# Four reorderings at the end of an attention and mixture-of-experts kernel: row scatters, lists, normalisations and token loads

## The chip, the cores and the metric

The kernel runs on one core of a Trainium2 chip. The metric is the device time of one launch in microseconds (us), the median of several runs. One further launch is recorded by the hardware profiler; all views of the profile are of that launch, and their times count from the start of its span.

## What is computed

The input is x, 4 sequences of 512 tokens with 256 features, and for each sequence 8 condition values. All is float32. Cut to what matters (c for the condition values):

```python
# one of 8 gated networks per sequence, chosen by the largest condition value
h = (silu(x @ wu.T + bu) * (x @ wg.T + bg)) @ wd.T + bd
# attention, 16 heads of width 16 that share one key and one value head
p = softmax(q @ k.T);  o = p @ v
x = x + o @ Wo.T + bo
# per sequence a weight mixed from 8 masked ones
z = x @ mix(c, weight * mask).T + bias
# routing in 8 groups of 256 tokens: each token goes to the best two of 8 experts,
# at most 128 places per expert and group; the rest is dropped
probs = softmax(z @ w_router);  top 2;  place = running count per expert
out = sum over a token's experts of probs * (gelu(z @ wi[e]) @ wo[e])
x = x + out
```

## The kernel before, in words

**Stages.** The first stage runs the gated networks for all sequences. The second walks through 64 steps n, 16 for each sequence b (k = n mod 16). A step computes four exponentiated score tiles on the scalar engine (`exponentials`, L409), takes the row maxima of a tile six steps ahead on the vector engine (`maxima`, L379), and multiplies the exponentials of the step before with the values (`weigh`, L423). Four steps make a unit of attention; its result is copied out of PSUM (L432) and stored to a buffer in memory, `od` (L433). The third stage runs the experts' networks.

**Work beside the attention steps.** The rest of a sequence is cut into pieces, which `finish(b)` builds and the lists `beside` and `last` hand out: entry k names the pieces of step k, with the sequence they belong to as an offset (-1 is the sequence before). `values` loads the attention results and their sums (L444, L448), `inv` takes the reciprocal (L473), stores it and loads it again spread over the partitions (L474, L478), `norm0` and `norm1` multiply (L486), `out0` to `out3` are the output projection with the residual (L503, L508, stored by L509), `rT` transposes (L524), `mix` multiplies with the mixed weight (L535), `choose` and `rank0`, `rank1` pick the two experts (L552 to L583), `places`, `rows` and `send` count places (L601 to L650). `row0` to `row3` each issue two scatters (L656): GpSimd DMAs that write 128 rows of 264 numbers to the places of `to_i` in a buffer `xp`, which is sorted by expert. In all but the last sequence a scatter also waits for the last `weigh` issued so far.

**Units of experts' work.** A unit is 256 rows of one expert (a pair) or 128 or fewer (singles and smaller ones). Which expert and which rows is known only at run time: `list_of_pairs` and `lists_of_rest` compute tables on the vector engine (L827 to L903), and SyncE reads them. The first two units come from the first two sequences, units 2 to 5 (N0 = 2 to NA = 6) after three, the rest after the last. For a unit u, `fetch_rows(u)` loads its rows from `xp` (L934), `fetch_in(u)` and `fetch_out(u)` its two weights of 1 MB (L912, three buffers each), `turn(u)` transposes the rows on the tensor engine (L978) and copies them back on the vector engine (L980), `up(u, half)` is the first product with gelu (L1051, L1055), `put(u, h)` the second (L1084), weighted by L1094 and added to the output by a GpSimd DMA (L1098). An add waits for the add of the unit before.

**What sets the order.** The program's text: each engine and each of SyncE's, ScalarE's and GpSimd's DMA queues executes in the order in which the instructions were written, and each instruction waits for the semaphores of what it depends on. So a SyncE load that waits for something holds up the loads written after it. `fetch_rows` of units 0 and 2 waits for all scatters so far, and that of the first unit of the rest for all of them.

**The passage from steps to units.** In the last sequence, `pairs0` to `pairs6` begin the third stage: `pairs2` loads unit 0's first weight and the rows of units 0 and 1, `pairs4` loads `fetch_in(1)` and `fetch_out(0)`, `pairs5` is `turn(0)`, `pairs6` is `fetch_in(2)` and `fetch_out(1)`. After the last step, `up(0, 0)` comes, then the last `weigh`, and `run(units, ..., begun=True)` takes over. In `run`, iteration k works on unit k's first product and unit k-1's second, loads rows of unit k+2 (`rows_behind`), `fetch_in` of unit k+3 and `fetch_out` of unit k+2. Between them it calls `place()`, and the n-th call does the pieces of the last sequence that `final` lists under n; `"rest"` there stands for `lists_of_rest`. Loads of units whose table isn't written yet are kept in `late` until it is.

Of the kernel before, what the change touches and what calls it, by code (L numbers as in the profile page):

```python
# [18 lines left out]
B = 4  # L19
# [17 lines left out]
N0, NA, NB, NSURE, NNEXT, NHALF, NQUARTER = 2, 6, 5, 10, 18, 2, 2  # L37
# [5 lines left out]
def adaln_attn_ffn_kernel(  # L43
# [22 lines left out]
    nc = tc.nc  # L66
    mm = nc.tensor.matmul
# [632 lines left out]
    def route_mixed(b):  # L700
# [39 lines left out]
    ]  # L740
    last = [
        [(-2, "rank0")],
        [(-2, "rank1")],
        [(-1, "values"), (-2, "places"), (-2, "rows")],
        [(-1, "inv"), (-2, "send")],
        [(-2, "row0")],
        [(-1, "norm0"), (-1, "norm1"), (-2, "row1")],
        [(-1, "out0"), (-1, "out1"), (0, "pairs0"), (-1, "out2"), (-1, "out3"), (-2, "row2")],
        [(-1, "rT0"), (-1, "rT1"), (-2, "row3")],
        [(-1, "mix0"), (-1, "mix1"), (0, "pairs1"), (-1, "mix2"), (-1, "mix3")],  # L750
# [1 line left out]
        [(-1, "rank1"), (0, "pairs2")],  # L752
        [(-1, "places"), (-1, "rows")],
        [(-1, "send"), (-1, "row0"), (0, "values0"), (0, "pairs3")],
        [(0, "pairs4"), (-1, "row1"), (-1, "row2")],
        [(0, "pairs5"), (-1, "row3")],
        [(0, "bias"), (0, "pairs6")],
    ]
    ON_PE = ("q", "k", "v", "out", "rT", "mix")

    final = {
# [4 lines left out]
    }  # L766
    LEAD = 6
    STEPS = 16 * B
# [46 lines left out]
    UQUARTER = UHALF + NE  # L815
# [50 lines left out]
    def list_of_pairs(u0, n):  # L866

        got = fp.tile([P, NE], F32, name="got", bufs=1)
        of_experts(got, -2.0 * P, ALU.is_ge, begin[:, :, 0:NG:2])
        if u0 > 0:  # L870
            nc.vector.tensor_tensor(got, got, pairs[:, 0:NE], ALU.subtract)
        end = ends_of_experts(got)
        yield
        list_of(u0, n, got, end, pairs, 2)

        room = fp.tile([P, NE], F32, name="room", bufs=1)
        nc.vector.tensor_tensor(room, got, end, ALU.subtract)
        nc.vector.tensor_scalar(room, room, float(n), 0.0, ALU.add, ALU.max)
        nc.vector.tensor_tensor(got, got, room, ALU.min)
        nc.vector.tensor_tensor(pairs[:, 0:NE], pairs[:, 0:NE], got, ALU.add)  # L880

    def lists_of_rest():
        for _ in list_of_pairs(NA, NB):
            pass
        got = fp.tile([P, NE], F32, name="got", bufs=1)
        twice = fp.tile([P, NE + 1], F32, name="twice", bufs=1)
        nc.vector.tensor_scalar(twice, pairs, 2.0, None, ALU.mult)
        most = fp.tile([P, 1], F32, name="most", bufs=1)
        nc.vector.memset(most, 0.0)
        for u0, n, less, sure in (  # L890
            (NA + NB, NTILE, -P / 2.0, NSURE), (UHALF, NE, -P / 4.0, NHALF),
            (UQUARTER, NE, 0.0, NQUARTER),
        ):
            of_experts(got, less, ALU.is_gt, begin)
            nc.vector.tensor_tensor(got, got, twice[:, 0:NE], ALU.subtract)
            end = ends_of_experts(got)
            list_of(u0, n, got, end, twice, 1)
            nc.vector.tensor_tensor(twice[:, 0:NE], twice[:, 0:NE], got, ALU.add)

            nc.vector.scalar_tensor_tensor(  # L900
                most, end[:, NE - 1 : NE], -float(sure), most, ALU.add, ALU.max
            )
        nc.vector.tensor_copy(count, most)  # L903

    wi_of, wo_of, xt_of, xT_of, hT_of = {}, {}, {}, {}, {}
    reg, adds, now = {}, [], []
# [22 lines left out]
    def fetch_rows(u):  # L929

        row = nc.sync.value_load(table[0:1, 0, u : u + 1], min_val=0, max_val=NE * EROWS)
        w = width(u)
        xt_of[u] = fp.tile([P, 2, XROW], F32, name="xt", bufs=4)
        i = nc.sync.dma_start(  # L934
            xt_of[u][:, 0:w], xp[ds(row, w * P), :].rearrange("(h p) c -> p h c", p=P)
        )
        if u in (0, N0) or (u >= NA and not first_of_rest):
            for k in scatters:
                tc.add_manual_dep(i.ins, k.ins.name, AFTER, reason="rows so far")
        if u < NA:  # L940
            tc.add_to_no_dep_group("first pairs", i.ins)
        else:
            first_of_rest.append(u)
# [3 lines left out]
    def first_pairs(part):  # L947
        if part == "0":
            parts.append(list_of_pairs(0, N0))
            next(parts[0])  # L950
        elif part == "1":
            next(parts[0], None)
        elif part == "2":
            fetch_in(0)
            fetch_rows(0)
            fetch_rows(1)
        elif part == "3":
            for _ in list_of_pairs(N0, NA - N0):
                pass
        elif part == "4":  # L960

            i = fetch_in(1)
            tc.add_manual_dep(i.ins, weighed[-1].ins.name, AFTER, reason="not at once")
            fetch_out(0)
        elif part == "5":
            turn(0, "x")
        else:
            i = fetch_in(2)
            tc.add_manual_dep(i.ins, weighed[-1].ins.name, AFTER, reason="not at once")
            fetch_out(1)  # L970

    def turn(u, tag="a"):

# [62 lines left out]
    def up(u, half):  # L1036

        if split(u) > 1:
            if half == 0:
                up_small(u)  # L1040
            return
        n = width(u) * P
        if half == 0:
            t = ep.tile([P, 4, 4, P], F32, name="e").rearrange("p a b t -> p (a b t)")
            hT_of[u] = t[:, 0 : F // P * n].rearrange("p (f t) -> p f t", f=F // P)
        each = 512 // n
        for f0 in range(4 * half, 4 * half + 4, each):
            ph = bank("m")
            for k in range(each):
                for c in range(2):  # L1050
                    mm(  # L1051
                        ph[:, ts(k, n)], wi_of[u][:, c, ts(f0 + k, P)], xT_of[u][:, c, :],
                        start=c == 0, stop=c == 1,
                    )
            nc.scalar.activation(  # L1055
                hT_of[u][:, f0 : f0 + each].rearrange("p f t -> p (f t)"), ph,
                AF.Gelu_apprx_tanh,
            )
# [109 lines left out]
    def place():  # L1168

        for name in final.get(next(places), ()):  # L1170
            if name == "rest":
                lists_of_rest()
                ready.update(range(NA, NUNIT))
                for f, u in late:
                    f(u)
                late.clear()
            else:
                work[B - 1][name]()

    ready, late = set(range(NA)), []  # L1180

    def fetch(f, u):

        if u in ready:
            f(u)
        else:
            late.append((f, u))

    def run(units, rows, begun=False):

        if not begun:
            turn(units[0])
        for k in range(len(units) + 1):
            for u in units[k : k + 1]:
                for x in rows(k):
                    fetch_rows(units[x])
                if begun and k == 0:
                    turn(units[1], "x")
                else:
                    up(u, 0)  # L1200
                if width(u) == 2:
                    place()
                up(u, 1)
                for x in units[k + 3 : k + 4]:
                    fetch(fetch_in, x)
                for x in units[k + 1 : k + 2]:
                    if not begun or k > 0:
                        turn(x)
                place()
            for u in units[k - 1 : k] if k else ():  # L1210
                for h in range(width(u)):
                    put(u, h)
                    place()
            for u in units[k : k + 1]:
                if split(u) > 1:
                    turn_small(u)
            for x in units[k + 2 : k + 3]:
                fetch(fetch_out, x)

    singles = range(NA + NB, NA + NB + NTILE)  # L1220
    by_half, by_quarter = range(UHALF, UQUARTER), range(UQUARTER, NUNIT)
# [4 lines left out]
        units += [*range(NA, NA + NB)[n : n + 1], *small[n : n + 1]]  # L1226

    def rows_behind(k):
        return (k + 2,) if k + 2 < len(units) else ()

    run(units, rows_behind, begun=True)
    left = nc.values_load(count[0:1, 0:1], min_val=0, max_val=NTILE)
# [93 lines left out]
```

## Time and profile before

| | |
|---|---|
| median of 3 runs | 650.72 us (650.18 to 651.39) |
| the profiled execution's own time | 648.59 us |
| its span | 646.9 us |
| TensorE matmul busy | 624.3 us |
| last matmul ends | 631.2 us |
| the attention steps end (end of the last `weigh`) | 381.98 us |
| first product of unit 0 begins | 377.26 us |
| transposes of unit 2 (L978) | 392.77 us |
| first product of unit 2 begins | 400.11 us |
| output projection of the last sequence (L503) begins | 403.56 us |
| lists of the rest on the vector engine | 435.00 to 451.42 us |
| first product of unit 5 begins | 452.51 us |

The timeline view gives one line for each instruction or run of equal ones: start, duration, engine, line, what it writes and reads, how many, and in brackets how long the engine was idle before and what ended that. A float32 matmul appears as two records. PE is the tensor engine, DVE the vector engine, ACT the scalar engine, POOL GpSimd, SP SyncE; a q behind the name is the engine's queue. The waits view gives for each line and releaser the total idle time, how often and the longest. For POOL's DMAs the duration is that of the issuing instruction, not of the transfer; when a transfer landed is read from the trace's records of semaphores.

### The profile page before, as it was taken

What the parts mean: (1) busy time and instruction counts of PE and PEld (TensorE: products, weight loads), DVE (VectorE), ACT (ScalarE), POOL (GpSimd) and SP (SyncE); (2) the same over time, 40 slices, a digit from 0 to 9 for tenths busy, and PEclk for the clock granted to TensorE, in tenths of its full rate; (3) what the DMA queues carried; (4) which work ended last, traced back from release to release, by engine and by line L of the source; (5) the groups of instructions that cost most, each with busy time, mean ns of one, the idle gap of its engine ahead of it and who ended that gap; (6) DMA issues with size and microseconds to landing.
All of it is one profiled execution on the core that took longest, in us unless ns stands there. A gap on an engine that the chain in (4) does not pass through costs nothing.

```text
span 646.9 us, 10162 instructions
## 1 busy us (share of the span) xinstructions
PE 624.3 (97%) x3736; PEld 364.0 (56%) x3736; DVE 335.2 (52%) x831; ACT 226.2 (35%) x404; POOL 111.3 (17%) x146
## 2 busy tenths in 40 slices
PE   8999999999999999999999989999999999999990
PEld 3444454333333433343335268887899999778880
DVE  1174844677768677876887744358222221322320
ACT  1212123566655555654653742221111111111220
POOL 1600000000000000310031141225332222313332
PEclk9999999999999999999999999999999999999996
DMA  7952981300142204321033399736889999888711
GB/s 234 358 167 72 310 269 34 98 19 18 34 132 68 67 18 117 135 68 48 19 121 100 130 334 271 237 99 208 233 275 317 323 333 315 254 275 264 209 20 19
DMA packets 65403, 107.11 MB, mean 166 GB/s; under 512 B 6914, under 2 KB 26946, under 8 KB 65346
## 3 DMA queue, kind: packets, MB, share of 16 engines
q1 hardware_dynamic: 50066, 87.96, 41.8%
q0 software_dynamic: 6400, 8.72, 6.7%
q10 hardware_dynamic: 8880, 9.71, 4.8%
q8 instruction: 31, 0.51, 0.3%
q14 instruction: 26, 0.21, 0.1%
HBM read 79.59 MB, written 26.65 MB: 164 GB/s over the span
## 4 chain that ended last, share of the span: by engine, by line
PE 91%; DMA 2%; DVE 2%; issue 1%; ACT 1%; POOL 1%; SPq 0%; POOLq 0%; DVEq 0%
PE ps_m L375 20%; PE ps_m L1051 17%; PE ps_x L1084 16%; PE ps_a L423 10%; PE ps_a L279 4%; PE ps_x L263 4%; PE ps_x L281 4%; PE ps_x L535 2%; PE ps_x L313 2%; PE ps_x L503 2%; PE ps_x L405 1%; PE ps_a L978 1%; PE ps_x L328 1%; PE ps_x L1018 1%; PE ps_m L995 1%
## 5 line engine op out<-in xcount | busy, mean ns | idle before, releaser
L379 DVE TENSOR_REDUCE negm<-ps_m 128x1 f32<-128x512 f32 x250 | 160.7, 686 | 63.1 <-PE ps_x L405 43.6
L409 ACT ACTIVATE e<-ps_x 128x512 f32<-128x512 f32 x244 | 132.5, 595 | 100.6 <-PE ps_x L405 96.9
L375 PE MATMUL ps_m<-k,q 32*128 32x512 f32 x500 | 153.3, 639 | 0.0
L405 PE MATMUL ps_x<-q,k 32*128 32x512 f32 x488 | 139.1, 639 | 0.0
L1051 PE MATMUL ps_m<-xT,wi_sb 128*128 128x256 f32 (+1 forms) x672 | 115.5, 330 | 3.2 <-issue 3.2
L1084 PE MATMUL ps_x<-wo_sb,e 128*128 128x256 f32 x512 | 114.3, 379 | 0.0
L1051 PEld LDWEIGHTS ps_m<-xT,wi_sb 128*128 128x128 f32 x672 | 103.6, 191 | 13.7 <-issue 4.5
L1084 PEld LDWEIGHTS ps_x<-wo_sb,e 128*128 128x128 f32 x512 | 95.6, 190 | 12.6 <-issue 0.4
L1055 ACT ACTIVATE e<-ps_m 128x512 f32<-128x512 f32 x64 | 38.0, 597 | 173.5 <-PE ps_m L1051 165.7
L375 PEld LDWEIGHTS ps_m<-k,q 32*128 32x128 f32 x500 | 46.5, 183 | 65.7 <-DVE negm L379 36.5
L1098 POOL DMA_INDIRECT out_dram<-y,to_row x36 | 55.5, 1542 | 136.9 <-DVE at L1074 31.6
L423 PE MATMUL ps_a<-e,v 128*32 128x256 f32 (+1 forms) x792 | 75.6, 454 | 0.6 <-ACT e L409 0.2
L423 PEld LDWEIGHTS ps_a<-e,v 128*32 128x32 f32 x792 | 15.6, 108 | 74.9 <-issue 62.5
L980 DVE COPY xT<-ps_a 128x256 f32<-128x256 f32 (+1 forms) x23 | 12.1, 528 | 81.0 <-PE ps_a L978 81.0
L1094 DVE TENSOR_SCALAR y<-ps_x,w 128x256 f32<-128x256 f32 x32 | 15.3, 482 | 58.5 <-PE ps_x L1084 58.5
L656 POOL DMA_INDIRECT xp<-x,to_i x32 | 33.1, 1036 | 55.7 <-DVE negm L379 25.1
L405 PEld LDWEIGHTS ps_x<-q,k 32*128 32x128 f32 x488 | 38.1, 183 | 0.2
L585 POOL TENSOR_SCALAR x<-mk 128x4 f32<-128x4 f32 x4 | 0.8, 211 | 205.4 <-DVE mk L582 205.3
L284 DVE SCALAR_TENSOR_TENSOR hid<-ps_x,wo_sb,sg 128x512 f32<-128x512 f32 x16 | 12.0, 749 | 45.5 <-PE ps_x L281 45.5
L279 PE MATMUL ps_a<-xT_sb,wi_sb 128*128 128x512 f32 x64 | 30.5, 599 | 0.4 <-DMA wi_sb<-in_wcond_dram 0.3
L281 PE MATMUL ps_x<-xT_sb,wi_sb 128*128 128x512 f32 x64 | 30.1, 592 | 0.0
L263 PE MATMUL ps_x<-hid,wo_sb 128*128 128x512 f32 x64 | 28.8, 597 | 0.0
(166 smaller groups left out, 465.1 us busy)
## 6 DMA issues: line engine op xcount, KB each, us to landing
wi_sb<-in_wi_dram SPq DMA_DIRECT2D x25, 1024.0 KB
wo_sb<-in_wo_dram SPq DMA_DIRECT2D x25, 1024.0 KB
xp<-zeros ACTq DMA_DIRECT2D x1, 8712.0 KB
q<-qd SPq DMA_DIRECT2D x8, 512.0 KB
wi_sb<-in_wcond_dram SPq DMA_DIRECT2D x15, 256.0 KB
od<-stage SPq DMA_DIRECT2D x15, 256.0 KB
xt<-xp SPq DMA_DIRECT2D x11, 264.0 KB
wo_sb<-in_wcond_dram SPq DMA_DIRECT2D x4, 517.0 KB
```

Of the source, the lines that this page charges most:

```text
L263: mm(po, wd[:, hc, ts(dc, P)], hid_of[b][:, hc, :], start=hc == 0, stop=hc == 3)
L279: mm(pu, wu[:, c, :], xT_sb[:, c, ts(b, T)], start=c == 0, stop=c == 1)
L281: mm(pg, wg[:, c, :], xT_sb[:, c, ts(b, T)], start=c == 0, stop=c == 1)
L375: mm(pm, q[32 * j : 32 * j + 32, i, ts(hg, P)], k[32 * j : 32 * j + 32, :], start=True, stop=True,)
L379: nc.vector.tensor_reduce(nm[:, i, j : j + 1], pm, AX.X, ALU.max, negate=True)
L405: mm(px, k[rows_j, ts(sc, P)], seqs[u // 4]["q"][rows_j, :, ts(u % 4, P)], start=True, stop=True,)
L409: nc.scalar.activation(e_of[n][:, :, j, :].rearrange("p h (i t) -> p i h t", i=4), px.rearrange("p (i h t) -> p i h t", i=4, h=4), AF.Exp,)
L423: i = mm(pa_of[u][32 * hh : 32 * hh + 32, j0 * P : (j0 + nj) * P], seqs[b]["v"][:, sc, :], e[:, hh, j0 : j0 + nj].rearrange("p j n -> p (j ...
L1051: mm(ph[:, ts(k, n)], wi_of[u][:, c, ts(f0 + k, P)], xT_of[u][:, c, :], start=c == 0, stop=c == 1,)
L1055: nc.scalar.activation(hT_of[u][:, f0 : f0 + each].rearrange("p f t -> p (f t)"), ph, AF.Gelu_apprx_tanh,)
L1084: mm(po[:, 0:D], hT_of[u][:, fc, ts(h, P)], wo_of[u][:, fc, :], start=fc == 0, stop=fc == F // P - 1,)
L1098: i = nc.gpsimd.indirect_dma_start(out=out_rows, out_offset=bass.IndirectOffsetOnAxis(ap=to, axis=0), in_=y, in_offset=None, compute_op=AL ...
```

## The change

1. **Normalisations.** In the last sequence `values` and `inv` come one step earlier in the list, and `norm0` and `norm1`, both in step 5 before, stand in steps 4 and 5. `rank1`, `send` and `row0` of the sequence before keep their steps.
2. **Scatters.** Of sequence 2, `row0` stays in step 12, `row1` goes from step 13 to 14, and `row2` and `row3` (steps 13 and 14) go behind the last step, to the first `place()` of `run`, written with a "-" ahead in `final`. They wait for the last `weigh`. The last products of `up(0, ...)` are put on the list of what scatters wait for too. Of the last sequence, `row0` stays under place 11, `row1` goes to 12, `row2` and `row3` to 13; GpSimd's adds of unit 2 now stand between them.
3. **Lists.** `lists_of_rest` becomes a generator of four parts: the pairs' list, the 39 single tiles, the halves and the quarters. One part is done in each of the places 12 to 15, and the loads kept in `late` go out as soon as their own part is written.
4. **Loads.** `pairs6` is dropped. In `run`, iteration 0 loads nothing. Iteration 1 begins with the rows of units 2 and 3, then `fetch_in(2)`, `fetch_out(1)`, `fetch_in(3)`, `fetch_out(2)`. Before, SyncE's order was `fetch_in(2)`, `fetch_out(1)`, rows of 2, `fetch_in(3)`, `fetch_out(2)`, rows of 3.

The order of instructions on the tensor engine and on the scalar engine is the same in both programs. The diff, cut to its core:

```diff
     last = [
         [(-2, "rank0")],
-        [(-2, "rank1")],
-        [(-1, "values"), (-2, "places"), (-2, "rows")],
-        [(-1, "inv"), (-2, "send")],
-        [(-2, "row0")],
-        [(-1, "norm0"), (-1, "norm1"), (-2, "row1")],
+        [(-1, "values"), (-2, "rank1")],
+        [(-2, "places"), (-2, "rows"), (-1, "inv")],
+        [(-2, "send")],
+        [(-1, "norm0"), (-2, "row0")],
+        [(-1, "norm1"), (-2, "row1")],
...
         [(-1, "send"), (-1, "row0"), (0, "values0"), (0, "pairs3")],
-        [(0, "pairs4"), (-1, "row1"), (-1, "row2")],
-        [(0, "pairs5"), (-1, "row3")],
-        [(0, "bias"), (0, "pairs6")],
+        [(0, "pairs4")],
+        [(0, "pairs5"), (-1, "row1")],
+        [(0, "bias")],
     ]
...
     final = {
-        0: ["inv0"], 2: ["values1"], 4: ["inv1", "norm0", "norm1"],
+        0: ["-row2", "-row3", "inv0"], 2: ["values1"], 4: ["inv1", "norm0", "norm1"],
...
-        11: ["places", "rows", "send", "row0", "row1", "row2", "row3"], 12: ["rest"],
+        11: ["places", "rows", "send", "row0"], 12: ["row1", "rest"], 13: ["row2", "row3", "rest"],
+        14: ["rest"], 15: ["rest"],
     }
...
     def lists_of_rest():
         for _ in list_of_pairs(NA, NB):
             pass
+        yield range(NA, NA + NB)
...
-        nc.vector.tensor_copy(count, most)
+            if u0 == UQUARTER:
+                nc.vector.tensor_copy(count, most)
+            yield range(u0, u0 + n)
...
-        elif part == "5":
+        else:
             turn(0, "x")
-        else:
-            i = fetch_in(2)
-            tc.add_manual_dep(i.ins, weighed[-1].ins.name, AFTER, reason="not at once")
-            fetch_out(1)
...
+            if u == 0:
+                weighed.append(i)
...
             if name == "rest":
-                lists_of_rest()
-                ready.update(range(NA, NUNIT))
+                ready.update(next(rest))
                 for f, u in late:
-                    f(u)
-                late.clear()
+                    if u in ready:
+                        f(u)
+                late[:] = [(f, u) for f, u in late if u not in ready]
+            elif name[0] == "-":
+                work[B - 2][name[1:]]()
...
+                if begun and k == 1:
+                    for n in (2, 3):
+                        fetch_in(units[n])
+                        fetch_out(units[n - 1])
...
                 for x in units[k + 3 : k + 4]:
-                    fetch(fetch_in, x)
+                    if not begun or k > 0:
+                        fetch(fetch_in, x)
...
             for x in units[k + 2 : k + 3]:
-                fetch(fetch_out, x)
+                if not begun or k > 0:
+                    fetch(fetch_out, x)
...
     def rows_behind(k):
-        return (k + 2,) if k + 2 < len(units) else ()
+        first = {0: (), 1: (2, 3)}
+        return first.get(k, (k + 2,) if k + 2 < len(units) else ())
```

More of the change, by code (lines that the diff above doesn't have):

```diff
@@ L1050, in up @@
                 for c in range(2):
-                    mm(
+                    i = mm(
                         ph[:, ts(k, n)], wi_of[u][:, c, ts(f0 + k, P)], xT_of[u][:, c, :],
@@ L1171, in place @@
             if name == "rest":
-                lists_of_rest()
-                ready.update(range(NA, NUNIT))
+                ready.update(next(rest))
                 for f, u in late:
-                    f(u)
-                late.clear()
+                    if u in ready:
[3 more added lines that the diff above has]
+                work[B - 2][name[1:]]()
             else:
                 work[B - 1][name]()
+    rest = lists_of_rest()
     ready, late = set(range(NA)), []
```

## The prediction

> **What bounds the kernel now.** I read the page first: how busy is TensorE, and what is the chain that ended last made of?
>
> ```profile
> span 646.9 us, 10162 instructions
> ...
> PE 624.3 (97%) x3736; PEld 364.0 (56%) x3736; DVE 335.2 (52%) x831; ACT 226.2 (35%) x404; POOL 111.3 (17%) x146
> ...
> PE 91%; DMA 2%; DVE 2%; issue 1%; ACT 1%; POOL 1%; SPq 0%; POOLq 0%; DVEq 0%
> ```
>
> TensorE bounds it. The change removes no matmul, so it can only win TensorE's waits. Of 22.5 us without a matmul some 1.9 lie at the start and 15.7 after the last one (631.2); the waits view of PE has the rest:
>
> ```profile
> PE ps_m L1051 <- issue: 3.2, 2, 2.1
> PE ps_x L503 <- issue: 0.8, 1, 0.8
> ```
>
> Third, the timeline about the larger of the two L1051 waits (start, duration, engine, line):
>
> ```profile
> 370.74 1.05 POOL L656 DMA_INDIRECT xp<-x,to_i  x1 [6.15 <-DVE cmp L835]
> ...
> 372.31 0.66 PE L978 MATMUL ps_x<-ident,xt 128*128 128x128 f32 x4
> ...
> 374.14 1.06 PE L423 MATMUL ps_a<-e,v 128*32 128x512 f32 x8
> ...
> 376.52 0.69 DVE L980 COPY xT<-ps_x 128x512 f32<-128x512 f32 x1 [3.04 <-PE ps_a L423]
> 376.62 0.60 ACT L409 ACTIVATE e<-ps_m 128x512 f32<-128x512 f32 x1 [3.09 <-PE ps_a L423]
> ...
> 377.24 1.95 POOL L656 DMA_INDIRECT xp<-x,to_i  x1 [0.30 <-issue]
> 377.26 3.72 PE L1051 MATMUL ps_m<-xT,wi_sb 128*128 128x256 f32 x16 [2.06 <-issue]
> ```
>
> The copy at 376.52 needs only the transposes that TensorE ended at 372.97, and DVE was free from 373.48. ACT stands still just as long. TensorE's own semaphore records come late here: 1.94 us for the matmuls ending at 372.38. Lags above 0.5 us lie almost only where POOL issues the scatters of L656, eight in a row here (370.74 to 381.77). Fourth, the other L1051 wait:
>
> ```profile
> 443.86 0.60 PE L978 MATMUL ps_a<-ident,xt 128*128 128x128 f32 x4
> ...
> 451.27 0.15 DVE L903 CAST count<-most 128x1 int32<-128x1 f32 x1
> 451.34 0.47 DVE L1094 TENSOR_SCALAR y<-ps_x,w 128x256 f32<-128x256 f32 x1
> 451.73 0.68 DVE L980 COPY xT<-ps_a 128x512 f32<-128x512 f32 x1
> ...
> 452.51 7.14 PE L1051 MATMUL ps_m<-xT,wi_sb 128*128 128x256 f32 x32 [1.15 <-issue]
> ```
>
> The transposes end at 444.46, but their copy stands on DVE behind all the last lists (435.00 to 451.42), and TensorE waits 1.15 us. Fifth, the chain at L503:
>
> ```profile
> 338.13 1.86 DVE attn L486 x2
> 339.99 0.04 issue
> 340.04 3.29 PE ps_x L503 x14
> ```
>
> TensorE was free at 338.45; the first L503 pair went ahead with half of attn, the other fourteen records waited for both normalisations.
>
> **What the skill says.** The Trainium skill, "SBUF — State Buffer", section "Who interferes with whom": a DVE instruction with two SBUF inputs contends with a GpSimd instruction that reads SBUF, and the one that issued second blocks. The trace agrees once: the scatter at 377.24 took 1.95 us, not 0.98, beside L494 (377.12 to 378.34). That doesn't explain the late signals, which come while DVE is idle. The skill's "DMA: Bandwidth & Descriptors", section "Anatomy of one DMA — SWDGE (gpsimd) path", gives 2.0 us plus bytes over 436 GB/s for a POOL DMA: an estimate of 2.3 us for a scatter's 135 KB; the one issued at 434.49, alone on the DMA engines, landed by the trace's records at 436.87, 2.4 us. Among weights' loads they took longer: 370.74 to 376.54. Section "Issuing engines are not separate DMA queues" of that page: all queues share 16 engines; here the DMA share is 1.06 at 376 to 378 us with both kinds under way.
>
> **The change part by part.** I call the end of the last L423 T: 381.98 before.
>
> PE's and ACT's orders are not changed by any part; DVE's, POOL's and SP's are.
>
> *Normalisations one per step.* Same DVE work in another order: only one L486 (0.93 us) stays between the transpose and L503. The inverse moves a step ahead: L473 goes from 329.76 to about 327.3 (sum landed at 326.26), so its reload, landed at 336.26, should land near 333.9, just where DVE is free (333.81) for the first L486. That fills the idle 0.94 before 334.75 and delays those reductions by some 0.1; the next pair has 0.53 of idle. SP's order there is unchanged. -0.93; bounds -1.0 and, if the reload is a microsecond late, -0.3.
>
> *Scatters.* The first four of sequence 2 stay about where they are, the third waiting a step longer; the last four move behind T. The first stall began with two or three issued, so four may be enough for it. For removal: in groups of two with 0.6 to 1.4 us between them (264 to 277), and in the row of four from 336.06, the late signals were at most about 1.0 us. With such a lag the copy would run by 374.7, before TensorE is free at 375.20, and the 2.06 would be gone. Bounds -2.06 and 0; I take -1.4, the middle of 0.7 and 2.06. Queued on POOL behind the moved scatters, which wait for T, are the first unit's adds; the first of them came at 398.12, T+16, so nothing clashes. In the last group the adds now stand between the pairs; TensorE doesn't wait there otherwise.
>
> *Last lists in four parts.* Some seventy small DVE instructions, the same work. Pairs' list 435.0 to 438.9, then y of L1094 (0.47), the 39-tile list (about 4.2) to 443.6, the third part (3.1, as at 447.99 to 451.08) to 446.7, then the copy: done by 447.5, needed at 451.37. Even 3 us of lag fit. -1.15; bounds -1.15 and 0. What is late next: the last four scatters of sequence 3 now stand behind two adds on POOL, 444 to 449, and the single's rows, issued at 449.67, move to about 453.5; landed near 456, they are needed for transposes at some 458.3.
>
> *The SP queue.* Before: third unit's wi and second's wo at 380.22 and 380.88, tokens at 389.25 after this wait:
>
> ```profile
> SPq L934 <- DMA xp<-x,to_i: 7.0, 3, 4.1
> ```
>
> After: two token loads, then wi, wo, wi, wo, all behind the last four scatters. Those start at T, issue every 1.29 us and land, at 2.4 each, by T+6.5. Tokens issue near T+7 and land by T+9.5 (transposes need them at T+10.8). The third wi issues at T+9.2. The wi issued at 390.46, beside the normalisation's two loads on ACT's queue, had the DMA engines from 392.5 and landed at 400.7: 8.2 us. So wi lands between T+15.5 and T+19; needed at 400.11, T+18.13. Its cover was 11.7 us and is now about one. I take +0.3; bounds 0 and +4.8 (below). A gain is excluded: tokens landed at 392.50, 0.27 before their transposes, so nothing waited for them.
>
> Sum: -0.93 - 1.4 - 1.15 + 0.3 = -3.2. The profiled execution took 648.59 (span 646.89 and 1.70 around it), so it would take 645.4; it lies 2.1 under the median 650.72, from which I subtract the same: 647.5.
>
> **Rivals.** *B, the late signals stay, or their gain is lost at the next wait:* -0.93 - 1.15 + 0.3 = -1.8, 648.9. For it: the stall starts with the first scatters and two 1 MB loads (372.74, 373.52), none of which is moved away. The second way: the last normalisation at 402.14 waits for o, with only 0.4 us before L503 at 403.56; if TensorE comes 2 us earlier and o doesn't, it waits there. *C, the moves give back what they gain* (late reload, a wait for wi of about 1.5): -0.3 - 1.15 + 1.5 = 0, 650.7. *D, slower, by SP's queue:* the last scatter of that group before took 8.3 us to land (380.79 to 389.04) among loads. If it does so again, tokens issue at T+12.3, wi at T+14.7, landed 8.2 later at T+22.9: TensorE waits 4.8. With the two sure gains 4.8 - 2.1 = +2.7, 653.4. It decides from about 3.4 us of wait, the last scatter landing after T+10.9. Against it: after the change no weights' load is issued between 373.5 and then, and those before were down by 383.8, T+1.8, so the engines should be free.
>
> **How the numbers follow.** This kernel can be told from no change at about 0.2%, 1.3 us. Forecast 0.48 (646.2 to 648.6), B 0.27 (648.3 to 649.8), C 0.11, D 0.14. Faster: 0.48, and three quarters of B, 0.20: 0.68. Same: the rest of B and most of C, and a little of D: 0.19. Slower: 0.13. The range runs from the forecast with all bounds (646.0, all of 2.06, no new wait) to 650.6, past B into C, leaving D and half of C.
>
> **What would show it.** Copy L980 of the first unit within a microsecond of its transposes and no L1051 wait before the last L423 (scatters); one L486 between transpose and L503 (normalisations); copy of the sixth unit by 448 (lists); no wait at the third unit's L978, L1051 or at L503 behind T (SP's queue). Wrong it is if TensorE's semaphores still come 2 us late with four scatters, or if L1051 of the third unit waits for wi.

## The result, and the profile after

The changed kernel took 647.71 us in the median of 13 runs (645.48 to 651.58), the kernel before 650.18 in 13 runs beside it (648.17 to 652.16): a ratio of 0.996, 95% interval 0.9942 to 0.9978, so faster: by 2.5 us between the medians. The profiled execution took 646.16 (span 644.4) against 648.59 (span 646.9). All lines below have shifted numbers: L978 to L980 are L980 to L982 now, L1051 is L1053, L1084 is L1088, L934 is L940, L912 is L918, L1098 is L1102. In some of the experiments they shift a little further.

TensorE's waits of the changed kernel (total, times, longest): neither L1051 "issue" nor L503 is among them. Two of the lines below are new: the wait for the third unit's first weight (L1053 for wi), and a short one for the row maxima (L375).

```profile
span 644.4 us, 10160 instructions
...
PE ps_x L93 <- DVE nil L91: 1.5, 1, 1.5
PE ps_m L1053 <- DMA wi_sb<-in_wi_dram: 1.0, 1, 1.0
PE ps_m L375 <- DVE negm L379: 0.3, 1, 0.3
```

The timeline of the changed kernel about the first unit's first product:

```profile
370.69 1.04 POOL L656 DMA_INDIRECT xp<-x,to_i  x1 [6.16 <-DVE cmp L837]
...
372.25 0.66 PE L980 MATMUL ps_x<-ident,xt 128*128 128x128 f32 x4
...
373.62 0.69 DVE L982 COPY xT<-ps_x 128x512 f32<-128x512 f32 x1 [0.19 <-PE ps_x L980]
373.79 0.98 POOL L656 DMA_INDIRECT xp<-x,to_i  x1 [0.77 <-PE ps_x L980]
...
375.08 3.72 PE L1053 MATMUL ps_m<-xT,wi_sb 128*128 128x256 f32 x16
```

The copy begins 0.71 us after the transposes end (372.91), where it began 3.55 after them, and L1053 waits for nothing. At the normalisations and at the sixth unit of the changed kernel:

```profile
335.04 1.05 DVE L486 TENSOR_TENSOR attn<-o,inv 128x512 f32<-128x512 f32 x1 [0.35 <-DMA inv<-ivd]
...
338.77 0.99 DVE L486 TENSOR_TENSOR attn<-o,inv 128x512 f32<-128x512 f32 x1
...
339.36 3.75 PE L503 MATMUL ps_x<-wo_sb,attn 128*128 128x256 f32 x16
...
446.04 0.68 DVE L982 COPY xT<-ps_a 128x512 f32<-128x512 f32 x1
...
450.21 7.07 PE L1053 MATMUL ps_m<-xT,wi_sb 128*128 128x256 f32 x32
```

One L486 is left in front of L503, and the sixth unit's copy is done 3.5 us ahead of its product. The third unit, behind T = 379.79 (end of the last L423):

```profile
386.62 1.54 SPq L940 DMA_DIRECT2D xt<-xp  x2
388.94 0.38 SPq L918 DMA_DIRECT2D wi_sb<-in_wi_dram  x1
389.51 0.61 SPq L918 DMA_DIRECT2D wo_sb<-in_wo_dram  x1
...
390.58 0.60 PE L980 MATMUL ps_a<-ident,xt 128*128 128x128 f32 x4
...
399.05 3.69 PE L1053 MATMUL ps_m<-xT,wi_sb 128*128 128x256 f32 x16 [0.96 <-DMA wi_sb<-in_wi_dram]
```

Tokens and wi were issued at T+6.8 and T+9.15, as forecast. The tokens come in time; wi landed at 398.91, T+19.1, and TensorE waits 0.96 for it.

TensorE's order is the same in both programs, so its starts can be compared instruction by instruction. The difference (after less before) in the two profiled executions, and what each stretch adds (the names in the last column say which part of the change lies in that stretch):

| at (time before) | difference | added here |
|---|---|---|
| 217.4, end of the networks and first steps | +0.58 | +0.58, nothing of the change lies there |
| 340.4, inside L503 | -0.22 | -0.80 normalisations |
| 377.26, first product of unit 0 | -2.19 | -1.97 scatters |
| 400.11, first product of unit 2 | -1.06 | +1.13 wait for wi |
| 452.51, first product of unit 5 | -2.30 | -1.24 lists |
| 631.20, end of the last matmul | -2.37 | -0.07 |

### The profile page after: what moved, and what is told of

It is laid out like the page before. It is cut to its first block, busy times and chain, and to the rows that moved or that the text cites. A ratio compares the mean times of both kernels' runs of the same rounds, so it can differ in the third digit from the quotient of the medians.

```text
span 644.4 us, 10160 instructions
## 1 busy us (share of the span) xinstructions
PE 625.3 (97%) x3736; PEld 364.9 (57%) x3736; DVE 335.0 (52%) x831; ACT 225.9 (35%) x404; POOL 110.5 (17%) x146
## 4 chain that ended last, share of the span: by engine, by line
PE 90%; DMA 4%; DVE 2%; issue 1%; POOL 1%; ACT 0%; SPq 0%; POOLq 0%; DVEq 0%
PE ps_m L375 21%; PE ps_m L1053 15%; PE ps_x L1088 15%; PE ps_a L423 9%; PE ps_a L279 4%; PE ps_x L263 4%; PE ps_x L281 4%; PE ps_x L535 2%; PE ps_x L313 2%; PE ps_x L503 2%; DMA wi_sb<-in_wi_dram 2%; PE ps_x L405 1%; PE ps_x L328 1%; PE ps_a L980 1%; PE ps_x L93 1%
## 5 line engine op out<-in xcount | busy, mean ns | idle before, releaser
L375 PE MATMUL ps_m<-k,q 32*128 32x512 f32 x500 | 153.8, 639 | 0.3 <-DVE negm L379 0.3
L1053 PE MATMUL ps_m<-xT,wi_sb 128*128 128x256 f32 (+1 forms) x672 | 115.5, 330 | 1.0 <-DMA wi_sb<-in_wi_dram 1.0
L1088 PE MATMUL ps_x<-wo_sb,e 128*128 128x256 f32 x512 | 114.3, 379 | 0.0
L1053 PEld LDWEIGHTS ps_m<-xT,wi_sb 128*128 128x128 f32 x672 | 103.6, 191 | 11.4 <-issue 2.2
L1088 PEld LDWEIGHTS ps_x<-wo_sb,e 128*128 128x128 f32 x512 | 95.6, 190 | 12.6 <-issue 0.4
L375 PEld LDWEIGHTS ps_m<-k,q 32*128 32x128 f32 x500 | 46.6, 183 | 66.4 <-DVE negm L379 36.8
L423 PE MATMUL ps_a<-e,v 128*32 128x256 f32 (+1 forms) x792 | 75.6, 454 | 0.5 <-ACT e L409 0.2
L1102 POOL DMA_INDIRECT out_dram<-y,to_row x36 | 55.7, 1548 | 113.9 <-DMA out_dram<-y,to_row 36.7
L423 PEld LDWEIGHTS ps_a<-e,v 128*32 128x32 f32 x792 | 15.6, 108 | 74.8 <-issue 62.5
L982 DVE COPY xT<-ps_a 128x256 f32<-128x256 f32 (+1 forms) x23 | 12.1, 528 | 81.5 <-PE ps_a L980 81.5
L1098 DVE TENSOR_SCALAR y<-ps_x,w 128x256 f32<-128x256 f32 x32 | 15.4, 482 | 58.8 <-PE ps_x L1088 58.8
```

The costliest lines, as they stand in the source:

```text
L375: mm(pm, q[32 * j : 32 * j + 32, i, ts(hg, P)], k[32 * j : 32 * j + 32, :], start=True, stop=True,)
L423: i = mm(pa_of[u][32 * hh : 32 * hh + 32, j0 * P : (j0 + nj) * P], seqs[b]["v"][:, sc, :], e[:, hh, j0 : j0 + nj].rearrange("p j n -> p (j ...
L1053: i = mm(ph[:, ts(k, n)], wi_of[u][:, c, ts(f0 + k, P)], xT_of[u][:, c, :], start=c == 0, stop=c == 1,)
L1088: mm(po[:, 0:D], hT_of[u][:, fc, ts(h, P)], wo_of[u][:, fc, :], start=fc == 0, stop=fc == F // P - 1,)
L1102: i = nc.gpsimd.indirect_dma_start(out=out_rows, out_offset=bass.IndirectOffsetOnAxis(ap=to, axis=0), in_=y, in_offset=None, compute_op=AL ...
```

## The experiments

The twelve runs fell, in order of time, on three chips: P (1 to 4 below), Q (5 and 6) and R (7 to 10 and a repeat of 3). On which chip the first comparison ran is not recorded, and the changed kernel itself was run again on Q alone. Each run is compared with the kernel before on its own chip: 645.59 us on P (37 runs), 648.83 on Q (21), 649.66 on R (35 runs) and, beside run 10, 649.96 (11).

**1. Normalisations alone**, in the kernel before:

```diff
-        [(-2, "rank1")],
-        [(-1, "values"), (-2, "places"), (-2, "rows")],
-        [(-1, "inv"), (-2, "send")],
-        [(-2, "row0")],
-        [(-1, "norm0"), (-1, "norm1"), (-2, "row1")],
+        [(-1, "values"), (-2, "rank1")],
+        [(-2, "places"), (-2, "rows"), (-1, "inv")],
+        [(-2, "send")],
+        [(-1, "norm0"), (-2, "row0")],
+        [(-1, "norm1"), (-2, "row1")],
```

> The kernel before with the normalisations one per step and nothing else. My theory: one L486 less stands between the last transpose and L503, so the fourteen records of L503 start 0.8 to 0.9 us earlier, no later wait takes that back, and the time falls by 0.8 (0.4 to 1.0). The rival: the gain is lost at the next wait (the gap of the first unit's L1051 at 377 grows by what was won, or the first L486 now waits for a later reload): no change, within 0.2 of the kernel before.

**2. Lists alone**, in the kernel before:

```diff
         11: ["places", "rows", "send", "row0", "row1", "row2", "row3"], 12: ["rest"],
+        13: ["rest"], 14: ["rest"], 15: ["rest"],
...
+        yield range(NA, NA + NB)
...
-        nc.vector.tensor_copy(count, most)
+            if u0 == UQUARTER:
+                nc.vector.tensor_copy(count, most)
+            yield range(u0, u0 + n)
...
-                lists_of_rest()
-                ready.update(range(NA, NUNIT))
+                ready.update(next(rest))
...
```

> The kernel before with the last lists in four parts and nothing else: all eight scatters of the last sequence stay in a row. My theory: the sixth unit's copy stands behind three parts of the lists in place of all of them and ends by 447.5 to 449.5 (the second figure if TensorE's signal comes 4.5 us late), so L1051 of that unit doesn't wait: -1.15. The rival: the late signals beside eight scatters hold the copy (or the lists) until TensorE is free at 451.4, and the lists' division needs the division of the scatters: 0 to -0.4.

Measured on P: normalisations 644.35, ratio 0.9974 (0.9963 to 0.9985); lists 645.00, ratio 0.9995 (0.9984 to 1.0006). In neither profile was a signal late. The normalisations gained 1.2 us between the medians, the lists nothing that can be told from noise. The timeline of the run with the normalisations:

```profile
373.62 3.72 PE L1051 MATMUL ps_m<-xT,wi_sb 128*128 128x256 f32 x16
...
390.43 0.66 PE L978 MATMUL ps_a<-ident,xt 128*128 128x128 f32 x4 [1.14 <-DMA xt<-xp]
...
397.83 3.62 PE L1051 MATMUL ps_m<-xT,wi_sb 128*128 128x256 f32 x16
...
448.92 7.07 PE L1051 MATMUL ps_m<-xT,wi_sb 128*128 128x256 f32 x32
```

and of the one with the lists:

```profile
338.34 4.07 PE L503 MATMUL ps_x<-wo_sb,attn 128*128 128x256 f32 x16 [0.81 <-DVE attn L486]
...
374.23 3.72 PE L1055 MATMUL ps_m<-xT,wi_sb 128*128 128x256 f32 x16
...
390.46 0.66 PE L982 MATMUL ps_a<-ident,xt 128*128 128x128 f32 x4 [0.56 <-DMA xt<-xp]
...
397.86 3.62 PE L1055 MATMUL ps_m<-xT,wi_sb 128*128 128x256 f32 x16
```

Both have eight scatters in a row, and neither has a wait at the first unit's product. The first has the lists undivided, and its sixth unit (448.92) doesn't wait either. So on this chip there was nothing for scatters or lists to win. The normalisations take away the 0.81 at L503 and are 0.61 ahead at 374, but the lead is gone at 397.8: the tokens, behind two weights' loads as in the kernel before, land no sooner, and the transposes wait 1.14 for them and not 0.56. By these two profiles the part alone would gain nothing there; by the interval the runs gained 1.0 to 2.4. That is not reconciled: each profile is one execution, and the kernel before was not profiled on P.

**3. Eight scatters in a row again**, in the changed kernel, run on P and later on R:

```diff
-        [(0, "pairs4")],
-        [(0, "pairs5"), (-1, "row1")],
+        [(0, "pairs4"), (-1, "row1"), (-1, "row2")],
+        [(0, "pairs5"), (-1, "row3")],
...
-        0: ["-row2", "-row3", "inv0"], 2: ["values1"], 4: ["inv1", "norm0", "norm1"],
+        0: ["inv0"], 2: ["values1"], 4: ["inv1", "norm0", "norm1"],
```

> The changed kernel with the scatters of sequence 2 as before: row1 and row2 in step 13, row3 in step 14, eight in a row from about 370.5, all else as changed. My theory (how many are issued in a row decides): TensorE's signal for the first unit's transposes comes about 2 us late again, the copy runs at about 376 and L1051 waits some 2 us for it; the third unit's wait for wi stays between 0 and 1. Time 2.06 above the changed kernel, that is some 0.5 below the kernel before. Its rival (the gap came from something else that the change moved, the loads' order or the normalisations' timing): L1051 still doesn't wait, some 2.5 below the kernel before.

> The changed kernel with eight scatters of sequence 2 in a row again, the same program as in the run before on the other chip, where no signal was late. On a chip with late signals, if their number decides: L1053 of the first unit waits about 2.0 us for its copy, and in some executions TensorE's clock is halved for 3.4 us after that: 2.0 to 3.6 above the changed kernel, near the kernel before. If the rest of the change removed the gap: no wait there, as the changed kernel.

On P: 644.64, ratio 0.9993 (0.9983 to 1.0004), and no gap, the rival's sign, though not for its reason:

```profile
370.92 0.66 PE L980 MATMUL ps_x<-ident,xt 128*128 128x128 f32 x4
...
372.01 0.68 DVE L982 COPY xT<-ps_x 128x512 f32<-128x512 f32 x1
...
373.75 3.72 PE L1053 MATMUL ps_m<-xT,wi_sb 128*128 128x256 f32 x16
```

On R the same program took 647.94, ratio 0.9973 (0.996 to 0.9986), 1.9 above run 7 below (the nearest to the changed kernel on that chip):

```profile
371.44 0.66 PE L980 MATMUL ps_x<-ident,xt 128*128 128x128 f32 x4
...
375.65 0.69 DVE L982 COPY xT<-ps_x 128x512 f32<-128x512 f32 x1 [3.05 <-remote]
...
376.40 3.72 PE L1053 MATMUL ps_m<-xT,wi_sb 128*128 128x256 f32 x16 [2.07 <-DVE xT L982]
```

From the end of the transposes to the copy it is 3.55 us here and 0.43 on P, for one program. So the late signals belong to the chip (or to what goes on in it at the time). Where they occur, the row of eight decides: on the same chip R, run 7, which has two scatters, a step's pause and two more, shows 0.69:

```profile
371.55 0.66 PE L980 MATMUL ps_x<-ident,xt 128*128 128x128 f32 x4
...
372.90 0.69 DVE L982 COPY xT<-ps_x 128x512 f32<-128x512 f32 x1 [0.18 <-PE ps_x L980]
```

**4. The third unit's wi ahead of the tokens**, at T:

```diff
+                if begun and k == 1:
+                    i = fetch_in(units[2])
+                    tc.add_manual_dep(i.ins, weighed[-3].ins.name, AFTER, reason="not at once")
                 for x in rows(k):
                     fetch_rows(units[x])
                 if begun and k == 1:
-                    for n in (2, 3):
-                        fetch_in(units[n])
-                        fetch_out(units[n - 1])
+                    fetch_out(units[1])
+                    fetch_in(units[3])
+                    fetch_out(units[2])
```

> The changed kernel with the third unit's wi issued ahead of the tokens, as soon as the last attention step is done; the other three loads stay behind the tokens. My theory: wi is issued some 9 us earlier and lands by about T+11, so the 0.96 us before the third unit's L1053 goes; the tokens' issue waits for the last scatter, which now lands beside one load and not two, so they land before T+10.8: 0.96 below the changed kernel, some 3.4 below the kernel before. The rival: the load holds the scatters up, the tokens land later than T+10.8 and the transposes wait for them as long as L1053 waited for wi: no change against the changed kernel, or slower by up to 1.

On P: 650.04, ratio 1.0062 (1.0044 to 1.0079), slower than the kernel before, and than run 3 on that chip. The rival's mechanism, and far beyond its price:

```profile
378.49 0.38 SPq L918 DMA_DIRECT2D wi_sb<-in_wi_dram  x1
388.38 1.54 SPq L940 DMA_DIRECT2D xt<-xp  x2
...
393.74 0.99 PE L980 MATMUL ps_a<-ident,xt 128*128 128x128 f32 x4 [4.37 <-DMA xt<-xp]
394.53 8.46 PE L1088 MATMUL ps_x<-wo_sb,e 128*128 128x256 f32 x32
```

One 1 MB load beside the scatters put the tokens' issue off from T+6.8 to T+10.0. After the wait L1088 took 8.46 us, not 7.07: TensorE's clock was halved for 3.41 us.

**5. Before and after again**, unchanged, on Q.

> The kernel before, unchanged, for a second profile: on the chip of the four runs so far it took 645.6 us and not 650.2, and no kernel there, the one with eight scatters in a row and the one with the lists undivided among them, showed a late signal of TensorE or a wait of L1051 for the copy. If the late signals belong to the program, both L1051 waits (2.1 and 1.2) are here again. My theory now is that they belong to the chip: where the time is about 645.6, TensorE waits before L503 (0.8) and for the third unit's tokens (0.5 to 1.1, L978) and nowhere at L1051; where it is about 650, the two L1051 waits are there.

> The changed kernel, unchanged, timed again. If its gain is the same on every chip: 2.5 below the kernel before. My theory now: without late signals the scatters and the lists gain nothing. What is left are the normalisations (0.8), the tokens' wait that goes (0.5 to 1.1) and the wait for wi that comes (1.0 to 1.3): 0.3 to 0.9 below the kernel before. On a chip with late signals 2.5 as in the first comparison.

Measured: the changed kernel 646.16 (8 runs), ratio 0.9952 (0.9932 to 0.9972), 2.7 us less than the 648.83 of the kernel before on this chip. The second profile of the kernel before shows the gap again. Its waits:

```profile
PE ps_m L1051 <- DVE xT L980: 2.0, 1, 2.0
...
PE ps_x L503 <- issue: 0.8, 1, 0.8
...
PE ps_m L1051 <- issue: 0.2, 1, 0.2
```

The first agrees with the first profile. The last one doesn't: the sixth unit waits 0.2 here and not 1.15, since the lists took 15.6 us and not 16.4 (14.9 on P). And the gap is followed by something new. The view below cuts the time into stretches and gives, for each, its length and the busy times of PE, PEld (weight loads), DVE, ACT and POOL with the number of instructions; the last three numbers are PE's granted clock, DMA share and GB/s:

```profile
376.00:377.00 1.00, 0.00 (x0) 0.00 (x0) 0.61 (x2) 0.51 (x2) 0.86 (x1) 1.00 1.05 363
377.00:378.00 1.00, 0.86 (x3) 0.68 (x4) 1.00 (x2) 0.58 (x2) 0.83 (x1) 0.68 1.03 383
378.00:379.00 1.00, 1.00 (x4) 0.81 (x3) 0.21 (x1) 0.46 (x1) 1.00 (x1) 0.50 1.03 398
...
381.00:383.00 2.00, 2.00 (x16) 1.17 (x14) 0.00 (x0) 1.47 (x2) 0.64 (x1) 1.00 1.08 382
```

TensorE gets half its clock for 3.41 us after a wait of 2.0, and the first unit's L1051 takes 5.41 us, not 3.72. The wait cost 3.7 in all. The Trainium skill, "TensorE: Matmul & The Clock Gate", section "Part 1: The HAM clock gate (the "warmup" mystery)", tells of such a gate with free-running windows of 3413 ns that halves the clock after an idle window; the length agrees, but 2.0 us of waiting were enough here, and the same gap of 2.06 in the first profile left the clock alone; the last section works out why. A halved window of 3.41 us takes 0.0026 off the mean granted clock of an execution of some 647 us. The profiles without one have means of 0.990 to 0.992, those with one 0.988 or 0.989, so the runs show roughly how often it happens: of the kernel before, 9 of 21 runs on Q lie below 0.990, and their median is 650.13 against 648.34; on R it is 17 of 35, 650.78 against 648.92; on P 2 of 37.

**6. wi in step 15**, in the changed kernel, as the kernel before has it; the three other loads behind the tokens:

```diff
-        [(0, "bias")],
+        [(0, "bias"), (0, "pairs6")],
...
+            i = fetch_in(2)
+            tc.add_manual_dep(i.ins, weighed[-1].ins.name, AFTER, reason="not at once")
...
-                    for n in (2, 3):
-                        fetch_in(units[n])
-                        fetch_out(units[n - 1])
+                    fetch_out(units[1])
+                    fetch_in(units[3])
+                    fetch_out(units[2])
```

> The changed kernel with the third unit's wi issued in step 15, behind the loads for the second unit, where the kernel before has it (about T - 4.5); the second's wo and the two other loads stay behind the tokens. My theory: the load lies ahead of the moved scatters and is down by about T+5, so the last scatters land as before and the tokens' issue stays at about T+6.8 (up to T+7.5); the wait of about 1.0 to 1.3 before the third unit's L1053 goes: 1.0 to 1.3 below the changed kernel. The rival: as with wi ahead of the tokens at T (which cost 4.4 us at the transposes), the load holds the scatters up and the tokens come after T+10.8: no gain, or slower than the changed kernel by up to 3.

On Q: 649.02, ratio 1.0011 (0.9992 to 1.0031), the gain lost, as the rival had it. wi went at 374.84 (T-4.6), the tokens only at T+8.8, and

```profile
393.29 1.11 PE L983 MATMUL ps_a<-ident,xt 128*128 128x128 f32 x4 [2.92 <-DMA xt<-xp]
394.20 8.06 PE L1091 MATMUL ps_x<-wo_sb,e 128*128 128x256 f32 x32
```

with a halved clock again. So in both places that were tried, step 15 and T, a 1 MB load ahead of the tokens makes them late once scatters stand behind T.

**7. wi between the tokens of units 2 and 3:**

```diff
...
+                    fetch_rows(units[2])
+                    fetch_in(units[2])
+                    fetch_rows(units[3])
+                    fetch_out(units[1])
+                    fetch_in(units[3])
+                    fetch_out(units[2])
...
```

> The changed kernel with the third unit's wi issued between the tokens of the third and of the fourth unit, in place of behind both: tokens of 2, wi of 2, tokens of 3, wo of 1, wi of 3, wo of 2. All still stand behind the last scatter. My theory: wi is issued about 1.2 us earlier (T+8.0 in place of T+9.2), lands as much earlier, and the wait of 1.0 before the third unit's L1053 goes; the first tokens were issued ahead of it and land as before: 1.0 below the changed kernel. The rival: wi's packets slow the tokens' down and TensorE waits for them at the third unit's L980, after T+10.8: no gain, and if that wait is 2 us or more, TensorE's clock may be halved for 3.4 us and the kernel is slower by 1 to 3.

On R: 646.03, ratio 0.9944 (0.9929 to 0.9959); the interval overlaps those of the changed kernel in the first comparison and on Q. wi was issued at T+8.0, 1.15 earlier, and still landed at T+19.1:

```profile
398.30 3.69 PE L1053 MATMUL ps_m<-xT,wi_sb 128*128 128x256 f32 x16 [0.91 <-DMA wi_sb<-in_wi_dram]
```

**8. The lists undivided**, in the changed kernel:

```diff
-        11: ["places", "rows", "send", "row0"], 12: ["row1", "rest"], 13: ["row2", "row3", "rest"],
-        14: ["rest"], 15: ["rest"],
+        11: ["places", "rows", "send", "row0"], 12: ["row1", "rest", "rest", "rest", "rest"],
+        13: ["row2", "row3"],
```

> The changed kernel with the last lists in one piece again, in place 12 behind row1; the scatters stay divided. If the division of the lists removed the sixth unit's wait: the copy stands behind all lists again and L1053 waits 0.2 to 1.2 us: as much above the changed kernel. The rival: the wait came from what the late signals add to the lists beside eight scatters (15.5 and 16.4 us for the lists there, 14.9 on the chip without late signals); with the scatters apart the lists take 14.9, the copy is done by about the time that TensorE gets there, and the time is that of the changed kernel, within 0.3.

On R: 652.89, ratio 1.0062 (1.0042 to 1.0081). Neither expectation gave the time. As the rival had it, the sixth unit didn't wait (lists 15.0 us, copy done at 449.18, product at 449.43). But:

```profile
439.74 0.23 POOL L1096 CAST to_row<-at 128x1 int32<-128x1 f32 x1
449.37 1.58 POOL L1102 DMA_INDIRECT out_dram<-y,to_row  x1 [9.40 <-DVE xT L982]
451.26 1.01 POOL L656 DMA_INDIRECT xp<-x,to_i  x1 [0.30 <-issue]
```

```profile
461.31 0.69 PE L980 MATMUL ps_a<-ident,xt 128*128 128x128 f32 x2 [4.81 <-DMA xt<-xp]
```

An add now stands between the scatters. It needs a y that DVE writes behind the lists (448.12 to 448.59; the view names the copy just behind it), and POOL stands still for 9.4 us. The last four scatters go out from 451.3 and not from 442.9 as in the first profile of the changed kernel, the next unit's tokens are 4.8 late, and the clock is halved for 6.83 us.

**9. Second unit's wi and first's wo a step earlier**, in the kernel before:

```diff
-        [(-1, "send"), (-1, "row0"), (0, "values0"), (0, "pairs3")],
-        [(0, "pairs4"), (-1, "row1"), (-1, "row2")],
+        [(-1, "send"), (-1, "row0"), (0, "values0"), (0, "pairs3"), (0, "pairs4")],
+        [(-1, "row1"), (-1, "row2")],
```

> The kernel before with the second unit's wi and the first's wo (1 MB each) issued a step earlier, in step 12, so that they start ahead of the eight scatters and not beside the second and third of them. If the start of the loads makes TensorE's signal late, the gap before the first unit's L1051 shrinks to under 0.7: 1.4 below the kernel before. If the eight scatters in a row do, the gap stays at about 2.0: within 0.3 of the kernel before. On a chip without late signals neither shows.

On R: 649.33, ratio 0.9992 (0.9976 to 1.0007), gap 2.02. It decides nothing: the loads went at T-9.2 and T-8.4, just where they went before (T-9.2, T-8.5), because SP takes them behind the loads of `values0` either way. What the loads contribute to the late signals stays open.

**10. The three other loads held back**, with the order of run 7:

```diff
                 up(u, 1)
+                if begun and k == 1:
+                    i = fetch_out(units[1])
+                    tc.add_manual_dep(i.ins, weighed[-1].ins.name, AFTER, reason="behind wi")
+                    fetch_in(units[3])
+                    fetch_out(units[2])
...
```

> The changed kernel with tokens of 2, wi of 2 and tokens of 3 behind the last scatter, and the three other weights' loads (wo of 1, wi of 3, wo of 2) held back until the second unit's first product is done, about T+10.8, where T+7.6 to T+12 was their issue. Issuing wi 1.2 us earlier alone didn't bring it in earlier: it landed at T+19 behind wo, wi and wo that were issued within 3.8 us of it. My theory: the four loads share the DMA engines and all end late, so wi alone is down by about T+15, the wait of 0.9 to 1.0 before the third unit's L1053 goes, and the later loads, needed from about T+30 on, cost nothing: 0.9 below the changed kernel, so 3.0 to 3.5 below the kernel before on a chip with late signals. The rival: wi is slow for another reason (the normalisation's small loads beside it), lands at T+18.5 or later all the same, and the time is that of the changed kernel.

On R: 644.74, ratio 0.9918 (0.9898 to 0.9938): below the kernel before by 5.2 us in the median. Its interval just overlaps that of run 7 (0.9929 to 0.9959), they were not run side by side, and the changed kernel itself was not run on R; so it is not shown that this run beats the changed kernel. The profile speaks against the theory:

```profile
398.91 3.69 PE L1053 MATMUL ps_m<-xT,wi_sb 128*128 128x256 f32 x16 [0.71 <-DMA wi_sb<-in_wi_dram]
```

wi's sixteen parts landed from 393.45 to 398.77. The last came at T+18.9, as the rival had it, although the next load was issued 3 us behind wi. So what lowers the time in this run is open. What holds the last parts up isn't settled either: the tokens' packets of 1 KB and the normalisation's two loads on ACT's queue lie beside it in all versions.

## Why the prediction was right, and where it was not

The time was forecast at 647.5 and came out at 647.71. That it is so close is luck: the kernel before took 650.18 in 13 runs and not 650.72, and the gain was 2.5 and not 3.2, two errors that nearly cancel. The profiled executions differ by 2.4, or 3.0 without the +0.58 that arose before the change begins, and there too a gain that was put too low (scatters) and a cost that was put too low (SP's queue) cancel. By its steps:

- *Normalisations, -0.93:* -0.80 in the profiles. The reload let the first L486 begin at 335.04, which is 0.6 later than it was put when the +0.58 of before is taken off; the later reductions cost TensorE 0.3 at L375.
- *Scatters, -1.4:* the mechanism holds and the term was too small. The whole gap went (-1.97; bound -2.06), because the remaining lag hides behind TensorE's other work. What the term left out is the clock: in some executions the gap costs about 1.7 more. On Q and R that went too, since none of the 8 runs of the changed kernel on Q and none of the 6 of run 7 on R lies below a mean clock of 0.990; in the first comparison 6 of 13 still do. That the gap would be there on every chip was assumed without saying so: on P no profile shows it, so there was nothing to gain.
- *Last lists, -1.15:* -1.24 in the profiles, but the cause was named only in part. Undivided lists make no wait of their own once the scatters stand apart (run 8), the kernel before waited 0.2 in its second profile, its order 0.8 in run 9, and on P there was no wait. The division is needed for another reason, which the prediction didn't see: it lets the add through that the change puts between the scatters.
- *SP's queue, +0.3:* a wait of 0.96 (+1.13 in the stretch), with the landing just past the end of what it gave (T+15.5 to T+19; it was T+19.1). The prediction had named L1051 of the third unit waiting for wi as a sign that it is wrong; by that sign this step was wrong. What failed is the size of the term, and "A gain is excluded ... so nothing waited for them". That held only while TensorE was late itself. With the first unit's gap gone, tokens behind two loads are what is late next: 0.56 and 1.14 on P in the order of before (runs 2 and 1). From the first unit's first product to the third's it is 24.21 us in run 1, with that order, and 24.30 in the run with eight scatters on P, with the new one: one wait stands in for the other.
- *Rival D* (tokens late behind the scatters) was put at 0.14. The mechanism is real, at 2.9 and 4.4 us plus the clock, but only with a weights' load beside the scatters, as the argument against it said.

So scatters, lists and loads are one change. On R, with late signals, the scatters bring about half of the gain: taking them back (run 3 on R) costs 1.9 of the 3.6 us that run 7 gains there, and the rest of the change brings the other 1.7. The order of loads and the divided lists keep the gain from being paid back: with wi back in step 15 it is 649.02 on Q, where the changed kernel takes 646.16, and with the lists undivided 652.89 on R, where run 7 takes 646.03. What the whole change gains on P wasn't measured; with the scatters in a row the rest of it gained nothing there that can be told from noise (run 3).

## What to carry to other kernels

When a wait is removed, redo the arrival times of everything behind it: a transfer that was in time by 0.27 us against a late consumer is the next wait. When work is put into gaps of an in-order queue, ask of each neighbour there what it waits for, as with the add that held four scatters back. And price a wait of TensorE of 2 us or more above its length, since in these traces the clock may be halved behind it.

## What was not expected of the hardware

TensorE's semaphores came late on Q, on R and in the first comparison, and not on P, with one program: 3.55 us against 0.43 from the transposes' end to the copy. In the traces with late signals some semaphore records are missing as well (863 of 869 of TensorE, 739 of 773 of DVE in the first profile), and in those of P none; whether one cause lies behind both, and whether the recording of the trace has a part in it, is open.

Waits of 2.0, 2.9, 4.4 and 4.8 us halved TensorE's clock for one or two windows of 3.41 us; waits of 2.06, 2.07 and 2.02 didn't. What tells them apart stands in the traces. Within each of the 14 traces all changes of the clock lie whole multiples of 3.41 us apart (in the second profile of the kernel before at 377.37, 380.78 and 636.78), so each trace can be cut into stretches of 3.41 us, whose place against the program differs from execution to execution. What counts is how long TensorE was idle inside one stretch:

| trace | wait | idle inside one stretch | clock in the next |
|---|---|---|---|
| run 3 on R | 2.07 | 1.21 | full |
| before, first profile | 2.06 | 1.70 | full |
| run 9 | 2.02 | 1.78 | full |
| before, second profile | 2.00 | 2.00 | half |
| run 6 | 2.92 | 2.40 | half |
| run 4 | 4.37 | 3.24 | half |
| run 8 | 4.81 | 3.41 | half, and in the one after |

Of all the stretches of the 14 traces that ran at the full clock, none with 1.95 us of idle time or less was followed by a halved one, and each with 2.00 or more was. So a gap of 2.0 us costs 1.7 more only when it falls whole into one stretch. If it falls at random, that is a share of (3.41 - 2.0) / 3.41 = 0.41 of the executions, an estimate from these figures; 9 of 21 on Q and 17 of 35 on R are 0.43 and 0.49.

In the first comparison 6 of the 13 runs of the changed kernel also lie at or below a mean clock of 0.989, and 5 of the 22 of run 3 on P, though their profiles show no wait over 1.3 behind the start; what those runs waited for was not recorded.
